# ConvNeXt block then selective scan on one core: the order of the loads between the first convolution and the MLP

## The chip, the cores and the metric

The kernel runs on one core of one Trainium2 chip, as one launch. The metric is the device time of that launch in microseconds; smaller is better. The time before the change is the median of three runs. A profile belongs to one further execution, which has its own time; the span in it runs from the first to the last instruction.

Names used below: TensorE (PE) multiplies matrices and PEld loads its weights, VectorE is DVE, ScalarE is ACT, GpSimd is POOL, and SP is SyncE, which issues most DMAs. A DMA moves data between the chip's main memory (DRAM here) and the on-chip memory; `SPq` in a profile is SP issuing one.

## The reference

The input `x` has 32 images of 96 channels and 56 x 56 pixels, float32. Two layers follow one another.

Layer 0 is a ConvNeXt block: a depthwise 7 x 7 convolution with bias, a layer norm over the 96 channels of each pixel, a small MLP (96 to 384, exact GELU, 384 to 96), a scale per channel, and the residual `+ x`:

```python
h = conv_depthwise_7x7(x) + conv_b                  # per channel
mu, var = mean(h, channels), var(h, channels)       # per pixel
h = (h - mu) * rsqrt(var + 1e-5) * ln_g + ln_b
h = gelu(h @ w1 + b1) @ w2 + b2                     # over channels
x = h * layer_scale + x
```

Layer 1 is a depthwise 5 x 5 convolution with SiLU, three small projections, and a scan along the 3136 pixels of each image with four states per channel. The change touches only layer 0.

## The kernel before

**Stages.** The kernel works in four stages with DRAM scratch tensors between them. *Convolution 1* goes over the 96 channels one by one; it writes the convolved rows to `conv1_d` and accumulates two statistics per pixel over the channels. *MLP* (the middle stage) goes over rows; it reads `conv1_d` and `x`, and writes `block_d`. *Convolution 2* goes over the channels again and writes `conv2_d`. *Scan* goes over images and halves of images.

**Layout.** The 32 images are two sets of 16. A row of a scratch tensor holds one image row of 16 images: 16 x 56 = 896 values (`COLS`). There are 2 x 56 = 112 such rows (`ROWS`), the first 56 for the first set. `conv1_d` is 96 channels x 112 rows x 896. The 896 are in two halves of 448 (`HALF`), the even and the odd pixels. `x` comes with the same rows, in pixel order.

**End of convolution 1.** For each channel after the first, `dt` is the difference to the first channel (L301); `acc1` sums it (L302) and `acc2` sums its square (L304), each 112 x 896. The statistics sit on 112 partitions as (half, row) and in the free dimension as (set of images, 448). After the last channel come L307 to L313: `sq` is `acc1` squared, `acc2` becomes the variance (L308, L311), ScalarE takes the root (L312, which loads an activation table first), and VectorE takes the reciprocal (L313). Two DMAs write it to `rstd_d` (L315), one for each half. The mean needs no step of its own: `w1` is centred when the weights are prepared.

**MLP.** The 112 rows are 28 groups of 4 (`RB`). A group needs seven tiles of three kinds: `r` is 1/std of its four rows, each row spread over 32 partitions (L345); `h` is the convolved rows for a block of 32 channels, with (row, channel) on 128 partitions and 896 in the free dimension, three blocks (L350); and `x` is the same piece of the input, loaded as four DMAs of one row each for every block (L354). So `load_rows` issues 1 + 3 + 12 DMAs. `normalise` multiplies one block of `h` by `r` in place on VectorE (L361). `hidden` is the first matrix product for one half of the pixels and 128 of the 384 hidden features (L371: 24 matmuls on 32-row tiles of the array) and GELU on ScalarE (L381). `result` is the second product (L390, 24 matmuls), to which VectorE adds bias and residual into the tile `o` (L401); after the second half POOL stores it to `block_d` with four DMAs (L413). Six `o` tiles are set to zero once at the start (L335), since a column of padding stays in them.

The loop runs over `k`, a half of a group at a time, with the second product one step behind the first. Loads run two groups ahead: groups 0 and 1 before the loop, group `n + 2` when `k` reaches group `n`. `h` and `x` have nine buffers each (three groups), `r` three.

**What sets the order.** A scheduler places instructions on each engine; those inside `pin(...)` keep the order of the program among themselves. In the MLP the normalises, matmuls and residual adds are pinned, the loads are not. In the built program SP has, for groups 0 to 2, `r`, then for each block `h` and four `x`; from group 3 on, the three `h` of a group, the `r` of the next group, and the twelve `x` of the group.

Waits come from two sources. A tile of a new pool stands on memory that the pool before has released, and waits for everything that used that pool. And SP's DMAs share eight semaphores in turn: a DMA waits, where needed, until the one eight places before it has landed.

The loads of `h` as the code has them:

```python
def rows_of(d, row, b):
    return d[CB * b : CB * b + CB, row : row + RB, :].rearrange("c r q -> r c q")
...
ht = pool.tile([128, COLS], F32, name=f"h_{n}_{d}", tag="h", bufs=9)
nc.sync.dma_start(ht, rows_of(conv1_d, row, d))
```

Of the kernel before, what the change touches and what calls it, by code (L numbers as in the profile page):

```python
# [8 lines left out]
F32 = mybir.dt.float32  # L9
AF = mybir.ActivationFunctionType  # L10
ALU = mybir.AluOpType
# [3 lines left out]
B, C, H, W = 32, 96, 56, 56  # L15
B2, BI = 2, 16
ROWS = B2 * H
COLS = BI * W
HALF = COLS // 2
# [20 lines left out]
RB = 4  # L40
# [6 lines left out]
def convnext_then_scan_kernel(  # L47
# [22 lines left out]
    nc = tc.nc  # L70
# [6 lines left out]
    conv1_d = dram.tile([C, ROWS, COLS], F32, name="conv1_d")  # L77
# [3 lines left out]
    rstd_d = dram.tile([ROWS, COLS], F32, name="rstd_d")  # L81
# [16 lines left out]
    eps_t = const.tile([128, 1], F32, name="eps_t")  # L98
# [42 lines left out]
    with tc.tile_pool(name="prep", bufs=1) as prep, tc.tile_pool(  # L141
        name="prep_ps", bufs=1, space=PSUM
# [8 lines left out]
        for i in range(3):  # L151
            for t in range(P1):
                j = 2 * t + 1 - i
# [11 lines left out]
        for k in range(QC):  # L165
            for f in range(QC):
                for t in range(2):
                    j = 4 * t + (k if k < 2 else k - 4) - f + K2 // 2
# [78 lines left out]
    def two(t):  # L247
        return t.rearrange("p (s q) -> p s q", s=2)

    with tc.tile_pool(name="c1", bufs=3) as pool, tc.tile_pool(  # L250
        name="c1k", bufs=1
    ) as keep, tc.tile_pool(name="c1_ps", bufs=4, space=PSUM) as psum:
        wts = [keep.tile([128, 2, H * P1], F32, name=f"wt1_{i}") for i in range(3)]
        xqs = [keep.tile([128, B2, BI, W2 + 3], F32, name=f"xq_{i}") for i in range(3)]
        for t in wts + xqs:
            nc.vector.memset(t, 0.0)
        first = keep.tile([ROWS, COLS], F32, name="first")
        acc1 = keep.tile([ROWS, COLS], F32, name="acc1")
        acc2 = keep.tile([ROWS, COLS], F32, name="acc2")
        nc.vector.memset(acc1, 0.0)  # L260
        nc.vector.memset(acc2, 0.0)

        def by_row(d, s):

            return d[:, s * PQ : (s + 1) * PQ].rearrange("(j m) q -> m j q", j=B2)

        for c in range(C):
            wv = toeplitz(taps1_d, wts[c % 3], K1, c, H)
            xt = pool.tile([128, COLS], F32, name=f"xt1_{c}", tag="xt")
            for j in range(B2):  # L270
                nc.sync.dma_start(xt[MP * j : MP * j + H], x[c, j * H : (j + 1) * H])

            xq = xqs[c % 3]
            for j in range(B2):
                xv = xt[MP * j : MP * j + H].rearrange("p (i r s) -> p s i r", i=BI, s=2)
                if j:
                    nc.vector.tensor_copy(xq[:H, j, :, 2 : W2 + 2], xv[:, 1])
                    nc.scalar.copy(xq[MP:KR, j, :, 1 : W2 + 1], xv[:, 0])
                else:
                    nc.gpsimd.tensor_copy(xq[:H, j, :, 2 : W2 + 2], xv[:, 1])  # L280
                    nc.scalar.copy(xq[MP:KR, j, :, 1 : W2 + 1], xv[:, 0])
            ps = psum.tile([ROWS, B2, 512], F32, name=f"ps1_{c}", tag="ps")
            for t in range(P1):
                for j in range(B2):
                    nc.tensor.matmul(  # L285
                        ps[:, j, :PQ].rearrange("p (i r) -> p i r", i=BI),
                        lhsT=wv[:KR, t],
                        rhs=xq[:KR, j, :, t : t + W2],
                        start=(t == 0),
                        stop=(t == P1 - 1),  # L290
                    )
            ht = first if c == 0 else pool.tile([ROWS, COLS], F32, name=f"ht_{c}", tag="ht")
            nc.scalar.activation(
                two(ht), ps[:, :, :PQ], AF.Identity, bias=c1b_t[:, c : c + 1], scale=1.0
            )
            for s in range(2):
                nc.gpsimd.dma_start(by_row(conv1_d[c], s), two(ht)[s * H : (s + 1) * H])
            if c:

                dt = pool.tile([ROWS, COLS], F32, name=f"dt_{c}", tag="dt")  # L300
                nc.vector.tensor_sub(dt, ht, first)  # L301
                nc.vector.tensor_add(acc1, acc1, dt)  # L302
                nc.scalar.activation(dt, dt, AF.Square)
                nc.vector.tensor_add(acc2, acc2, dt)  # L304

        sq = keep.tile([ROWS, COLS], F32, name="sq")
        nc.vector.tensor_mul(sq, acc1, acc1)  # L307
        nc.vector.scalar_tensor_tensor(  # L308
            acc2, in0=sq, scalar=-1.0 / C, in1=acc2, op0=ALU.mult, op1=ALU.add
        )  # L310
        nc.vector.tensor_scalar(acc2, acc2, 1.0 / C, 0.0, ALU.mult, ALU.max)  # L311
        nc.scalar.activation(acc2, acc2, AF.Sqrt, bias=eps_t[:ROWS], scale=1.0)  # L312
        nc.vector.reciprocal(acc1, acc2)  # L313
        for s in range(2):
            nc.sync.dma_start(by_row(rstd_d, s), two(acc1)[s * H : (s + 1) * H])  # L315

# [1 line left out]
    with tc.tile_pool(name="mlp", bufs=2) as pool, tc.tile_pool(  # L321
        name="mlp_h", bufs=3, space=PSUM
    ) as ps_h, tc.tile_pool(name="mlp_o", bufs=2, space=PSUM) as ps_o:
        pin = tc.keep_in_program_order
        blocks = C // CB
# [6 lines left out]
            pool.tile([128, QC, BI, QP], F32, name=f"o_{i}", bufs=1) for i in range(2 * blocks)  # L332
        ]
        for t in ots:
            nc.vector.memset(t, 0.0)  # L335

        def rows_of(d, row, b):
            return d[CB * b : CB * b + CB, row : row + RB, :].rearrange("c r q -> r c q")

        def load_rows(n):  # L340
            row = n * RB
            j, m = divmod(row, H)
            rt = pool.tile([128, COLS], F32, name=f"r_{n}", tag="r", bufs=3)
            rts[n] = rt
            nc.sync.dma_start(  # L345
                rt, bass.AP(rstd_d.tensor, rstd_d.offset + row * COLS, [[COLS, RB], [0, CB], [1, COLS]])
            )
            for d in range(blocks):
                ht = pool.tile([128, COLS], F32, name=f"h_{n}_{d}", tag="h", bufs=9)
                nc.sync.dma_start(ht, rows_of(conv1_d, row, d))  # L350
                hts[n, d] = ht
                xt = pool.tile([128, COLS], F32, name=f"x_{n}_{d}", tag="x", bufs=9)
                for i in range(RB):
                    nc.sync.dma_start(  # L354
                        xt[CB * i : CB * i + CB],
                        x[CB * d : CB * d + CB, j * H + H - 1 - m - i, :],
                    )
                xts[n, d] = xt

        def normalise(n, d):  # L360
            pin(nc.vector.tensor_mul(hts[n, d], hts[n, d], rts[n]))  # L361
# [56 lines left out]
        parts = groups * 2  # L418
        load_rows(0)
        load_rows(1)  # L420
        for d in range(blocks):
            normalise(0, d)
        for k in range(parts + 1):
            n = k // 2
            if k % 2 == 0 and n + 2 < groups:
                load_rows(n + 2)
            for f in range(3):
                if k < parts:
                    hidden(n, k % 2, f)
                if k:  # L430
                    result((k - 1) // 2, (k - 1) % 2, f)
                if k % 2 and n + 1 < groups:
                    normalise(n + 1, f)

# [335 lines left out]
```

## Time and profile before

| | |
|---|---|
| time, median of 3 runs | 3781.97 us (3781.74 to 3783.92) |
| the profiled execution, its own time | 3784.25 us |
| its span | 3782.4 us |
| granted TensorE clock, mean over the span | 0.824 |
| busy share: PE, DVE, ACT, POOL | 81, 74, 57, 60% |
| loads of `h` from `conv1_d` | 84 of 448 KB each |
| loads of `x` in the MLP | 336 of 112 KB each |
| loads of `r` from `rstd_d` | 28 of 448 KB each |

How to read it: a share of busy time is a mean over four stages with different limits. The page's slices (40 of 94.6 us) show them: TensorE is busiest up to about 1490 us, the end of the MLP, and VectorE after it. The timeline lists instructions in order of time with start, length, engine, line, operation, tiles (`out<-in`), and in brackets the idle time before it and what ended that wait. The line numbers are those of the kernel before. Busy time counts what the profile has for an engine; issuing a DMA isn't counted.

### The profile page before, as it was taken

The numbers are of one execution on the slowest core, as the hardware profiler recorded it, in microseconds if no ns is written. First come the engines' busy times: TensorE is split into PE (matmuls) and PEld (weight loads), VectorE is DVE, ScalarE is ACT, GpSimd is POOL, SyncE is SP. The second block draws the span as 40 slices with busy tenths as digits, with TensorE's granted clock in tenths as the row PEclk, the third lists the DMA queues.
The fourth block names the chain that finished last, engine by engine and source line by source line (L and its number), as shares of the span: only waits on it lengthen the run. The fifth ranks groups of instructions, "written<-read, shape, count | busy, mean of one in ns | idle before, by whom it ended". The sixth has DMA issues, their size and how long they took to land. (4 is left out here: it accounts for less than half of the span.)

```text
span 3782.4 us, 46657 instructions
## 1 busy us (share of the span) xinstructions
PE 3068.1 (81%) x17290; PEld 1274.2 (34%) x17290; DVE 2788.7 (74%) x1865; ACT 2169.2 (57%) x2037; POOL 2275.0 (60%) x1433
## 2 busy tenths in 40 slices
PE   7999995999999998876746777777777777787774
PEld 5777773333333333322212222222222222222221
DVE  5666664233333333999976999999999999999998
ACT  3555552333333333222217888888888878888884
POOL 2333331122222222677756898999889989988996
PEclk9999997999999999999976667666666666666666
DMA  5555553455555552877758877787778778777873
GB/s 155 165 168 168 165 168 102 153 170 162 159 159 161 164 163 79 228 215 216 217 137 274 273 257 263 267 277 252 260 273 272 253 264 274 267 259 261 276 252 113
DMA packets 303015, 790.71 MB, mean 209 GB/s; under 512 B 123972, under 2 KB 181124, under 8 KB 278116
## 3 DMA queue, kind: packets, MB, share of 16 engines
q1 hardware_dynamic: 252356, 630.77, 51.1%
q0 software_dynamic: 36096, 118.41, 11.4%
q10 hardware_dynamic: 14336, 38.54, 2.6%
q8 instruction: 137, 2.24, 0.2%
q14 instruction: 90, 0.74, 0.1%
HBM read 551.83 MB, written 235.74 MB: 208 GB/s over the span
## 5 line engine op out<-in xcount | busy, mean ns | idle before, releaser
L652 POOL TENSOR_TENSOR hs<-hs,ct 128x1568 f32<-128x1568 f32 x192 | 672.6, 3503 | 104.2 <-DVE hs L641 91.0
L625 POOL TENSOR_TENSOR rep<-rep,bt 128x1568 f32<-128x1568 f32 x192 | 674.5, 3513 | 13.6 <-DMA rep<-du_d 13.6
L381 ACT ACTIVATE g<-ph,b1p_t 128x896 f32<-128x896 f32 x336 | 320.3, 1004 | 512.4 <-PE ph L371 512.4
L401 DVE SCALAR_TENSOR_TENSOR o<-po,b2r_t,x 128x224 f32<-128x224 f32 x336 | 190.6, 609 | 572.7 <-PE po L390 572.7
L413 POOL DMA_DIRECT2D block_d<-o x336 | 183.1, 552 | 709.0 <-DVE o L401 621.9
L285 PE MATMUL ps<-xq,wt 120*112 120x448 f32 x1536 | 581.2, 540 | 14.3 <-POOL xq L280 14.3
L371 PE MATMUL ph<-h,w1r_t 32*128 32x448 f32 x4032 | 440.9, 560 | 60.2 <-DVE h L361 58.9
L285 PEld LDWEIGHTS ps<-xq,wt 120*112 120x112 f32 x1536 | 429.9, 280 | 165.2 <-POOL xq L280 14.5
L489 DVE COPY st<-yt 28x896 f32<-28x896 f32 x288 | 437.3, 1518 | 16.3 <-ACT yt L483 10.8
L556 PE MATMUL pz<-xs,wd_t 96*96 96x392 f32 x512 | 279.3, 712 | 187.8 <-ACT du L564 135.3
L472 PE MATMUL ps<-xq,wt 128*32 128x448 f32 x3072 | 311.3, 549 | 126.3 <-ACT yt L483 114.1
L390 PE MATMUL po<-g,w_t 128*32 128x448 f32 x4032 | 413.1, 543 | 0.0
L665 PE MATMUL py<-hs,sel_t 128*32 128x392 f32 x1536 | 330.1, 685 | 83.0 <-POOL hs L652 83.0
L632 DVE TENSOR_TENSOR_SCAN pv<-rep,pv 128x1568 f32<-128x1568 f32 x96 | 329.1, 3428 | 61.8 <-ACT rep L621 53.5
L601 PE MATMUL pk<-bn,pick_t 8*128 8x392 f32 x1024 | 290.1, 691 | 98.5 <-ACT y L675 80.7
L637 DVE SCALAR_TENSOR_TENSOR pv<-pv,rep 128x1568 f32<-128x1568 f32 x192 | 345.6, 1800 | 20.7 <-POOL hs L652 0.9
L632 DVE TENSOR_TENSOR_SCAN pv<-rep,carry_p,pv 128x1568 f32<-128x1568 f32 x96 | 334.9, 3489 | 9.8 <-DVE hs L641 1.3
L641 DVE TENSOR_TENSOR_SCAN hs<-rep,carry_h,pv 128x1568 f32<-128x1568 f32 x96 | 334.1, 3480 | 10.4 <-DVE pv L637 0.5
L641 DVE TENSOR_TENSOR_SCAN hs<-rep,pv 128x1568 f32<-128x1568 f32 x96 | 328.3, 3420 | 9.9 <-DVE pv L637 0.5
L619 ACT ACTIVATE rep<-rep,a_t 128x1568 f32<-128x1568 f32 x192 | 308.3, 1606 | 9.8 <-DMA rep<-du_d 9.4
L658 PE MATMUL py<-xs,dsm_t 96*96 96x392 f32 x512 | 304.9, 738 | 9.8 <-ACT ct L605 4.5
L620 ACT ACTIVATE rep<-rep,lift_t 128x1568 f32<-128x1568 f32 x192 | 307.6, 1602 | 6.3
(88 smaller groups left out, 3532.0 us busy)
## 6 DMA issues: line engine op xcount, KB each, us to landing
rep<-du_d SPq DMA_DIRECT2D x192, 1568.0 KB
du_d<-du SPq DMA_DIRECT2D x128, 588.0 KB
xq<-block_d SPq DMA_DIRECT2D x192, 225.0 KB
block_d<-o POOLq DMA_DIRECT2D x336, 120.0 KB, 5.7
xt<-in_x_dram SPq DMA_DIRECT2D x192, 196.0 KB
h<-conv_d SPq DMA_DIRECT2D x84, 448.0 KB
x<-in_x_dram SPq DMA_DIRECT2D x336, 112.0 KB
conv_d<-st POOLq DMA_DIRECT2D x96, 392.0 KB, 4.7
```

The costliest lines, as they stand in the source:

```text
L285: nc.tensor.matmul(ps[:, j, :PQ].rearrange("p (i r) -> p i r", i=BI), lhsT=wv[:KR, t], rhs=xq[:KR, j, :, t : t + W2], start=(t == 0), stop ...
L371: pin(nc.tensor.matmul(phs[i // 2][:, i % 2, :HALF], lhsT=w1r_t[rows, d, f * 128 : (f + 1) * 128], rhs=hts[n, d][rows, s * HALF : (s + 1) ...
L381: nc.scalar.activation(gt, ph[:, :, :HALF], AF.Gelu, bias=b1p_t[:, f : f + 1], scale=1.0)
L390: pin(nc.tensor.matmul(po[CB * i : CB * i + CB, :HALF], lhsT=w2_t[:, f, CB * d : CB * d + CB], rhs=gts[n, s, f, i // 2][:, i % 2], start=( ...
L472: nc.tensor.matmul(ps[RW * f : RW * f + RW, h, : B * QW].rearrange("p (b q) -> p b q", q=QW), lhsT=wv[:, f, t], rhs=xv[:, :, t : t + QW], ...
L489: copy(st[:, :, :, :, f], yt[RW * f : RW * f + QR].rearrange("p h (b q) -> p h b q", q=QW),)
L625: pin(nc.gpsimd.tensor_mul(ut, ut, bts[i // NG]))
L632: pin(nc.vector.tensor_tensor_scan(run, da, zero, carry_p[:, col : col + 1] if q else 1.0 / EPS, ALU.mult, ALU.add))
L637: pin(nc.vector.scalar_tensor_tensor(run, in0=run, scalar=1.0, in1=ut, op0=ALU.min, op1=ALU.mult))
L641: pin(nc.vector.tensor_tensor_scan(ht, da, run, carry_h[:, col : col + 1] if q else 0.0, ALU.mult, ALU.add))
L652: pin(nc.gpsimd.tensor_mul(ht, ht, cts[k]))
L665: pin(nc.tensor.matmul(py[g * DG : (g + 1) * DG, s, :BK], lhsT=sel_t, rhs=hss[k * NG + g][:, cols], start=False, stop=True, tile_position= ...
```

## The change

- `acc1` and `acc2` move to a pool of their own, `stats`, which stays open until the MLP is done (`front.close()`).
- `load_rows` now issues only the three `h` of a group. A new function `load_more` issues `r` and the twelve `x`. All these DMAs are pinned.
- `load_rows(0)` and `load_rows(1)` come first, then the norm's last steps, which are now in the MLP's pool (`sq` is a tile of it), then `load_more(0)` and `load_more(1)`. In the loop `load_more` follows `load_rows`.
- The reciprocal is taken in two halves of the free dimension, one for each set of 16 images. Each half is written to `rstd_d` with two DMAs, pinned: four in all.
- The zeroing of the `o` tiles moves from VectorE to POOL.

```diff
+    front = ctx.enter_context(ExitStack())
+    stats = front.enter_context(tc.tile_pool(name="stats", bufs=1))
+    acc1 = stats.tile([ROWS, COLS], F32, name="acc1")
+    acc2 = stats.tile([ROWS, COLS], F32, name="acc2")
...
-        acc1 = keep.tile([ROWS, COLS], F32, name="acc1")
-        acc2 = keep.tile([ROWS, COLS], F32, name="acc2")
...
-        sq = keep.tile([ROWS, COLS], F32, name="sq")
-        nc.vector.tensor_mul(sq, acc1, acc1)
-        nc.vector.scalar_tensor_tensor(
-            acc2, in0=sq, scalar=-1.0 / C, in1=acc2, op0=ALU.mult, op1=ALU.add
-        )
-        nc.vector.tensor_scalar(acc2, acc2, 1.0 / C, 0.0, ALU.mult, ALU.max)
-        nc.scalar.activation(acc2, acc2, AF.Sqrt, bias=eps_t[:ROWS], scale=1.0)
-        nc.vector.reciprocal(acc1, acc2)
-        for s in range(2):
-            nc.sync.dma_start(by_row(rstd_d, s), two(acc1)[s * H : (s + 1) * H])
...
-            nc.vector.memset(t, 0.0)
+            nc.gpsimd.memset(t, 0.0)
...
         def load_rows(n):
+            row = n * RB
+            j, m = divmod(row, H)
+            for d in range(blocks):
+                ht = pool.tile([128, COLS], F32, name=f"h_{n}_{d}", tag="h", bufs=9)
+                pin(nc.sync.dma_start(ht, rows_of(conv1_d, row, d)))
+                hts[n, d] = ht
+
+        def load_more(n):
             row = n * RB
             j, m = divmod(row, H)
             rt = pool.tile([128, COLS], F32, name=f"r_{n}", tag="r", bufs=3)
             rts[n] = rt
-            nc.sync.dma_start(
+            pin(nc.sync.dma_start(
                 rt, bass.AP(rstd_d.tensor, rstd_d.offset + row * COLS, [[COLS, RB], [0, CB], [1, COLS]])
-            )
+            ))
             for d in range(blocks):
-                ht = pool.tile([128, COLS], F32, name=f"h_{n}_{d}", tag="h", bufs=9)
-                nc.sync.dma_start(ht, rows_of(conv1_d, row, d))
-                hts[n, d] = ht
                 xt = pool.tile([128, COLS], F32, name=f"x_{n}_{d}", tag="x", bufs=9)
                 for i in range(RB):
-                    nc.sync.dma_start(
+                    pin(nc.sync.dma_start(
                         xt[CB * i : CB * i + CB],
                         x[CB * d : CB * d + CB, j * H + H - 1 - m - i, :],
-                    )
+                    ))
                 xts[n, d] = xt
...
         load_rows(0)
         load_rows(1)
+
+        sq = pool.tile([ROWS, COLS], F32, name="sq", bufs=1)
+        nc.vector.tensor_mul(sq, acc1, acc1)
+        nc.vector.scalar_tensor_tensor(
+            acc2, in0=sq, scalar=-1.0 / C, in1=acc2, op0=ALU.mult, op1=ALU.add
+        )
+        nc.vector.tensor_scalar(acc2, acc2, 1.0 / C, 0.0, ALU.mult, ALU.max)
+        nc.scalar.activation(acc2, acc2, AF.Sqrt, bias=eps_t[:ROWS], scale=1.0)
+        for i in range(B2):
+
+            nc.vector.reciprocal(acc1[:, i * HALF : (i + 1) * HALF], acc2[:, i * HALF : (i + 1) * HALF])
+            for s in range(2):
+                pin(nc.sync.dma_start(
+                    rstd_d[i * H : (i + 1) * H, s * HALF : (s + 1) * HALF],
+                    acc1[s * H : (s + 1) * H, i * HALF : (i + 1) * HALF],
+                ))
+        load_more(0)
+        load_more(1)
...
             if k % 2 == 0 and n + 2 < groups:
                 load_rows(n + 2)
+                load_more(n + 2)
...
+
+    front.close()
```

## The prediction

> **What bounds the kernel now.** I read the page's busy slices, then the timeline across the seam between the first convolution and the MLP, then the busy table by stretches. On the page:
>
> ```profile
> span 3782.4 us, 46657 instructions
> ...
> PE   7999995999999998876746777777777777787774
> ...
> PEclk9999997999999999999976667666666666666666
> ```
>
> A slice is 94.6 us. The MLP (about 671 to 1490 us) runs TensorE at 9 or more; the dip to 5 with a clock of 7 is the seam, at 567 to 662 us. The change acts there. The timeline of the seam (start, length, engine, line; the bracket is the idle time before and what ended it):
>
> ```profile
> 613.32 1.09 DVE L304 TENSOR_TENSOR acc<-acc,dt 112x896 f32<-112x896 f32 x1
> ...
> 618.65 5.75 DVE L313 RECIPROCAL acc<-acc 112x896 f32<-112x896 f32 x1 [2.45 <-ACT acc L312]
> 624.43 0.75 SPq L315 DMA_DIRECT2D rstd_d<-acc  x2
> 627.63 0.63 SPq L345 DMA_DIRECT2D r<-rstd_d  x1
> ...
> 641.95 1.09 DVE L361 TENSOR_TENSOR h<-h,r 128x896 f32<-128x896 f32 x1 [8.15 <-DMA h<-conv_d]
> ...
> 648.92 1.09 DVE L361 TENSOR_TENSOR h<-h,r 128x896 f32<-128x896 f32 x1 [5.88 <-DMA h<-conv_d]
> ...
> 655.78 1.09 DVE L361 TENSOR_TENSOR h<-h,r 128x896 f32<-128x896 f32 x1 [5.77 <-DMA h<-conv_d]
> ...
> 656.93 3.35 PE L371 MATMUL ph<-h,w1r_t 32*128 32x448 f32 x12 [4.99 <-DVE h L361]
> ...
> 658.87 1.28 ACT L381 ACT_TABLE_LOAD   x1 [40.26 <-PE ph L371]
> ...
> 661.22 7.44 PE L371 MATMUL ph<-h,w1r_t 32*128 32x448 f32 x48 [0.94 <-ACT g L381]
> ...
> 671.50 2.46 PE L390 MATMUL po<-g,w_t 128*32 128x448 f32 x24
> ```
>
> Read: the last matmul of the convolution ends at 608.9; the norm's chain ends with the reciprocal at 624.40; two writes of 1/std land by 627.6; then r, h (from 628.31) and x (from 628.90) of group 0 are issued. The three normalised blocks of group 0 wait for DMA until 641.95, 648.92 and 655.78, and only then can GELU begin (658.87). So the last 30 us of the seam are transfer time, and the norm only sets when the transfers start. The busy table, with columns PE, PEld, DVE, ACT, POOL (busy and count), clock, DMA share, GB/s:
>
> ```profile
> 741.00:747.00 6.00, 5.46 (x56) 1.85 (x56) 2.13 (x3) 1.91 (x2) 0.00 (x0) 1.00 0.25 95
> ```
>
> In this stretch h loads issued at 739.0 are on their way: a share of 0.25 at 95 GB/s is four of sixteen DMA engines at 24 GB/s each. From 671 us on no normalise waits for a DMA: a group takes 29.97 us (714.8 to 744.8 for the third block), its loads are issued 6 us and more ahead at first, 20 to 50 us later.
>
> **The Trainium skill.** *DMA: Bandwidth & Descriptors*, section "Why a DMA increments its semaphore by 16 and not by 1": a DMA issued from SP runs on k engines, k the largest number up to 16 that divides the slowest dimension of both patterns, and takes the lowest-numbered k; the other 16-k increments come at once. An h load has 128 partitions on one side and `r c q` with 4 rows outermost on the other: k = 4. r likewise 4; x (32 and 32) 16; the new 1/std writes (56 and 56) 14. The trace agrees: in its semaphore records h of block 0 has one early record (629.3) and just four late ones, 641.3 to 641.9; an x load has twelve records near 632.5 and four at 641.5 to 642.1; a 1/std write has fourteen. Same page, "Queues, rings and completion order": SP owns one ring on each engine, consumed in ring order. The trace agrees: those four late records of x come right after the h issued before it. *TensorE: Matmul & The Clock Gate*, Part 1: half clock until about one busy window of 3.4 us. Here the clock was 0.50 from 612.0 to 666.6, and the window from 663.2 was the first without a gap.
>
> **Part by part.** The changed program's order and waits, which can be read from its build, are used beside the durations above.
>
> 1. *h of groups 0 and 1 first.* Six h loads go to SP ahead of the 1/std writes. The first waits for the release of the convolution's pool: the last accumulate (ends 614.41) and the last conv1_d stores (records up to 613.9). So it issues at 614.5. All six use the same four engines. A load is 458,752 bytes: 4.6 us at 100 GB/s, 4.8 at the 95 above. With a start-up of 1.7 us (estimate, from the first landing record of the 1/std write, 626.2, after its issue at 624.43) the six end at 616.2 + 6 x 4.7 = 644.4. Nothing else competes then. Before, h and r of group 0 alone cost 9.4 (r_0, 627.63 to its last record at 637.0) + 4.9 + 7.0 + 6.9 us, the x loads between them included.
>
> 2. *The norm's steps later, with sq in the new pool.* sq was done in the shadow of the square (612.28); it now follows the last accumulate: +1.1 us. Two reciprocals of half length, 2.9 us each by 5.75/2. Chain: sq 614.5, L308's step 615.6, L311's 616.7, table load and sqrt 617.4 to 619.7, halves end at 622.7 and 625.6. Nothing waits for this (next point): there are 18 us of cover. Without that cover the 1.1 us would count, and the first half would give 2.9 us back.
>
> 3. *The 1/std writes, now four.* They stand behind six h loads in the rings of engines 0 to 3. Each brings 4 descriptors per engine (0.3 us), so the first two land about 1 us after the last h: 645.5, not 625.2. The halves buy nothing, since the second pair sits in the ring as well, ahead of r_0 on SP.
>
> 4. *r_0, then x.* r_0 waits for the first two writes: issue 645.6. Then 12 x. Up to seven x go out at once behind it, since SP's DMA semaphores come round every eight loads and the ones needed have landed. That is as before, when five or six x ran beside r_0 and it took 9.4 us; without disturbance 1.7 + 4.7 = 6.4. So r_0 lands between 652.0 and 655.0; I take 654.0, near the measured case.
>
> 5. *Start of the MLP.* All three h of group 0 have long landed, so the normalises follow at once (1.09 us each) and TensorE runs 24 matmuls without a gap: 8 cold ones took 1.88 us (timeline at 643.25 and 650.07), so 1.1 + 3 x 1.88 = 6.7 us. GELU's table load comes at 660.7, against 658.87: +1.8 us. In return the clock rises sooner: TensorE is busy without a gap from 655.1, so a full window is done by 658.6 to 662, not 666.6. Before, from 661.22 to 666.6, it did at half clock what takes half the time, 2.7 us too many; the GELU chain (0.95 us each, three PSUM buffers) hides part of it. I count -2.3 us. Sum at the first output matmul: +1.8 - 2.3 = -0.5 us; with r_0 at 652.0 it is -2.5.
>
> 6. *Later loads.* x_0 lands by 657, needed at about 674. r_1 comes behind 12 x: issue about 658, landing 665, needed at 675. h of group 2: issue 667, needed at 705. Nothing late.
>
> 7. *Steady groups.* Before, SP already ran h, then r of the next group, then x; now r of the same group follows h. It is needed over 20 us later: nothing. Pinning changes no more.
>
> 8. *Memsets of o on POOL.* On DVE they took 0.86 us each, six, in the wait for h. The timeline has no POOL entry from 612 to 691 us, so they find the engine free; even at several us each they end long before 674. What they may hold up on DVE is covered by the 18 us of point 2. Both ends nothing.
>
> Sum: -0.5 us, so span 3782. The profiled execution took 3784.25 beside its span, 2.3 above the median of 3781.97, so against the median: 3781.5.
>
> **Rivals.** *A, the queue takes the gain* (above): -4 to +5 us by the two bounds of h (4.6 or 4.9) and of r_0 (6.4 or 9.4). *B, faster: the transfers do overlap the norm.* If the h loads spread over sixteen engines, or the rings didn't hold the 1/std writes back, r_0 would issue at about 628 to 630, when the first three h are in, and land by 634 to 639; GELU starts 13 to 18 us sooner: 3764 to 3769. For it: the chain of waits then has only the norm in it. Against: four late records, 95 GB/s, and x landing behind h. A half-way case, with writes early but r_0 behind h of group 1: r_0 at 650, -4 us, within A. *C, slower: the h loads run below 100 GB/s,* so that 1/std is held longer. The price is six times the excess; from 5.9 us per load it passes the bound: 616.2 + 35.4 + 1.2 + 9.4 = 662.2, 8 us over A. For it: in the steady groups an h with its share of x and stores takes about 6 us. Against: here no x or store runs beside them. Price at 6.2 us: +10, so 3792. *D, the change does nothing* because the h loads stay behind the norm: excluded by the order, they stand first on SP.
>
> **How the numbers follow.** A 0.76, B 0.15, C 0.08, D 0.01. About 0.2% (7.6 us) is what a measurement of this kernel can tell from no change. Faster: B, 0.15. Slower: C, 0.08, and a little of A's tail, 0.09. Same: 0.76. The forecast is A's. A alone gives 3777 to 3787; B and C together are 0.23, and to leave out no more than 0.2 the range goes a little into both: 3772 to 3788.
>
> **What would show it.** Right: the six h loads issue from 614.5, and r_0 only at 644 to 647; the three normalises of group 0 follow each other without a gap at 652 to 656; DMA share near 0.25 at 95 to 105 GB/s through 618 to 644; first output matmul within 3 us of 671.5; clock up before 664. Wrong: r_0 issued before 635 (B), or a DMA share of 0.5 and more while h loads run. If normalises of group 1 or 2 wait for r, point 6 fails.

## The result, and the profile after

The changed kernel takes 3785.74 us (median, 3783.18 to 3787.97); the kernel before, run beside it on the same chip, 3782.30 us (3780.03 to 3787.0). The ratio is 1.0007, with a 95% interval of 0.9999 to 1.0015. That interval just includes no change, so this measurement doesn't tell one, though a loss of a few us is likelier than a gain. The forecast was 3781.5 us, "same" with 0.76. The profiled execution took 3786.44 us, its span is 3784.6 us. The page's lines that correspond to those shown of before:

```profile
span 3784.6 us, 46641 instructions
...
PE   7999994999999998876746777777777777777775
...
PEclk9999997999999999999976667666766776666666
```

The dip to 4 and a clock of 7 still stand in the same slice, the seam between the first convolution and the MLP. The timeline of that seam (start, length, engine, line of the changed kernel; in brackets the idle time before and what ended it):

```profile
615.51 13.57 SPq L336 DMA_DIRECT2D h<-conv_d  x6
615.64 5.56 POOL L326 MEMSET o<- 128x960 f32 x6 [3.09 <-DVE acc L306]
616.04 1.09 DVE L419 TENSOR_TENSOR sq<-acc 112x896 f32<-112x896 f32 x1 [0.66 <-DVE acc L306]
...
618.30 1.23 DVE L423 TENSOR_SCALAR acc<-acc 112x896 f32<-112x896 f32 x1
...
621.97 5.76 DVE L427 RECIPROCAL acc<-acc 112x448 f32<-112x448 f32 x2 [2.45 <-ACT acc L424]
629.13 6.33 SPq L429 DMA_DIRECT2D rstd_d<-acc  x4
646.51 0.52 SPq L344 DMA_DIRECT2D r<-rstd_d  x1
...
656.81 3.09 DVE L357 TENSOR_TENSOR h<-h,r 128x896 f32<-128x896 f32 x3 [29.08 <-DMA r<-rstd_d]
658.11 4.95 PE L367 MATMUL ph<-h,w1r_t 32*128 32x448 f32 x28 [48.24 <-DVE h L357]
...
662.45 1.28 ACT L377 ACT_TABLE_LOAD   x1 [40.51 <-issue]
...
664.81 4.23 PE L367 MATMUL ph<-h,w1r_t 32*128 32x448 f32 x24 [1.75 <-ACT g L377]
...
674.59 2.46 PE L386 MATMUL po<-g,w_t 128*32 128x448 f32 x24
```

The three waits for `h` of before (until 642, 649 and 656 us) have become one wait of 29.08 us for `r`, and it ends at 656.81, 1.0 us later than the last of the three did. The reciprocal's halves end at 624.9 and 627.7; `r` of group 0 isn't issued until 646.51, because the last parts of the 1/std writes land only then. The busy table by stretches, with columns PE, PEld, DVE, ACT, POOL (busy and count), clock, DMA share, GB/s:

```profile
622.00:628.00 6.00, 0.00 (x0) 0.00 (x0) 5.73 (x2) 0.00 (x0) 0.00 (x0) 0.50 0.26 103
628.00:634.00 6.00, 0.00 (x0) 0.00 (x0) 0.00 (x0) 0.00 (x0) 0.00 (x0) 0.50 0.27 108
634.00:640.00 6.00, 0.00 (x0) 0.00 (x0) 0.00 (x0) 0.00 (x0) 0.00 (x0) 0.50 0.38 147
640.00:646.00 6.00, 0.00 (x0) 0.00 (x0) 0.00 (x0) 0.00 (x0) 0.00 (x0) 0.50 0.25 102
```

From 622 to 646 us a quarter of the DMA engines is busy, at 102 to 108 GB/s, but for one stretch. The trace's semaphore records, which note when each engine has finished its part of a DMA, have the six `h` loads landing at 623.7, 628.2, 632.6, 637.1, 641.5 and 646.0, one every 4.45 us. Each 1/std write has fourteen parts. Ten of them land from 634.5 to 636.8, on engines that carry no `h` load; they are what is more in the stretch with 0.38 and 147 GB/s. The other four parts come only at 645.7 to 647.0, right behind the sixth `h`. *DMA: Bandwidth & Descriptors* of the Trainium skill, "Queues, rings and completion order", says that an engine consumes the descriptors (the single moves) of a ring, its queue for one issuing engine, in order; this is what it looks like when a small write stands behind six large loads.

### The profile page after: what moved, and what is told of

Read it like the earlier page. It is cut to its first block, busy times and chain, and to the rows that moved or that the text cites. A ratio compares the mean times of both kernels' runs of the same rounds, so it can differ in the third digit from the quotient of the medians.

```text
span 3784.6 us, 46641 instructions
## 1 busy us (share of the span) xinstructions
PE 3056.8 (81%) x17290; PEld 1269.7 (34%) x17290; DVE 2783.8 (74%) x1860; ACT 2168.5 (57%) x2037; POOL 2279.8 (60%) x1439
```

## Theory, rivals, and how the runs are read

The theory, that of the forecast: the change moves the `h` loads into the shadow of the norm, but all six use the same four DMA engines, and the writes of 1/std and then `r` stand behind them there. The rivals: the norm's chain is what ends last (then halves, memsets and the order of its steps matter); or loads of this kind are slow whatever engines they use.

One measure is used for all profiles below, since it leaves out the rest of the kernel: *the seam*, from the end of the last convolution matmul to the first output matmul (`po`). It is 62.60 us before (608.90 to 671.50) and 64.72 us after (609.87 to 674.59). From `po` to the end a profile has 3106.5 to 3111.5 us, in no order that follows the edits. That, and stage one (the first convolution) ending anywhere from 608.3 to 610.3, is why whole times of variants that differ by 1 to 2 us are not told apart here.

| kernel | time, us | before beside it | ratio, 95% | `r_0` issued | first normalise | seam |
|---|---|---|---|---|---|---|
| before | 3781.97 | | | 627.63 | 641.95 | 62.60 |
| changed | 3785.74 | 3782.30 | 0.9999 to 1.0015 | 646.51 | 656.81 | 64.72 |
| h of group 0 alone ahead | 3770.65 | 3781.82 | 0.9956 to 0.9981 | 632.92 | 643.67 | 51.62 |
| writes by ScalarE | 3781.57 | 3781.82 | 0.9989 to 1.0006 | 629.77 | 652.26 | 60.81 |
| split loads | 3760.52 | 3781.82 | 0.9929 to 0.9958 | 628.36 | 632.67 | 42.15 |
| one reciprocal | 3783.76 | 3781.82 | 0.9996 to 1.0014 | 645.92 | 655.38 | 63.55 |
| zeroing on VectorE | 3782.51 | 3781.57 | 0.9994 to 1.0011 | 644.39 | 654.03 | 63.34 |
| r of two groups ahead of x | 3782.91 | 3781.57 | 0.9995 to 1.0013 | 645.78 | 655.38 | 63.93 |
| r, then h of group 2, then x | 3781.17 | 3781.68 | 0.9990 to 1.0008 | 646.61 | 653.87 | 61.39 |
| early GELU table | 3780.77 | 3781.68 | 0.9991 to 1.0008 | 645.48 | 656.21 | 62.56 |
| before, with split loads | 3767.45 | 3782.11 | 0.9945 to 0.9975 | 628.05 | 634.14 | 47.97 |
| split, h of group 0 alone ahead | 3757.77 | 3782.11 | 0.9919 to 0.9953 | 626.34 | 630.26 | 39.08 |
| the same, one reciprocal | 3760.53 | 3782.11 | 0.9930 to 0.9959 | 630.38 | 634.45 | 41.15 |
| the same, zeroing on VectorE | 3762.91 | 3782.11 | 0.9933 to 0.9963 | 632.21 | 636.18 | 44.42 |

`r_0` is `r` of group 0, and so on.

## Is it the queue?

**Only h of group 0 ahead.** A shorter queue in front of the writes, nothing else:

```diff
         load_rows(0)
-        load_rows(1)
...
         load_more(0)
+        load_rows(1)
         load_more(1)
```

> Edit: the changed kernel, but only the three h loads of group 0 stand ahead of the norm; those of group 1 follow the x loads of group 0. Ring theory (1/std waits in SP's rings for every h load issued before it, 4.45 us each as in the changed kernel): three h loads fewer ahead, so r_0 issues at about 633 instead of 646.5, lands at 643.5, GELU's first table load comes at about 649 instead of 662.5; r of group 1 then lands at about 666 and may be 1 to 2 us late for its normalise. Time about 12 us under the changed kernel: 3774. Rival (the first two groups' bytes over four engines set the start, whatever the order): group 1 waits for what group 0 gains; time within 4 us of the changed kernel's 3785.7.

Measured: 3770.65 us. The timeline of this kernel:

```profile
621.86 5.76 DVE L426 RECIPROCAL acc<-acc 112x448 f32<-112x448 f32 x2 [2.45 <-ACT acc L423]
624.85 3.55 SPq L428 DMA_DIRECT2D rstd_d<-acc  x4
632.92 0.52 SPq L344 DMA_DIRECT2D r<-rstd_d  x1
...
643.67 3.10 DVE L357 TENSOR_TENSOR h<-h,r 128x896 f32<-128x896 f32 x3 [16.04 <-DMA r<-rstd_d]
...
661.37 2.46 PE L386 MATMUL po<-g,w_t 128*32 128x448 f32 x24
...
669.97 1.09 DVE L357 TENSOR_TENSOR h<-h,r 128x896 f32<-128x896 f32 x1 [4.86 <-DMA r<-rstd_d]
```

Three loads fewer in the queue are 3 x 4.45 = 13.4 us; `r_0` is issued 13.6 us sooner than in the changed kernel, and the seam is 13.1 us shorter. The norm's steps stand as they did. So the queue set the end, not the norm, and this part of the theory holds. The last line shows the price: `r_1` now comes late, and group 1 waits 4.86 us. That costs next to nothing: from the first to the last output matmul this kernel takes 828.1 us, the kernel before 828.0. The time came out 3.4 us under what the theory gave.

**The writes from another queue.** The four writes are issued by ScalarE, whose queue has nothing else in this stretch; all six `h` stay ahead:

```diff
-                pin(nc.sync.dma_start(
+                pin(nc.scalar.dma_start(
                     rstd_d[i * H : (i + 1) * H, s * HALF : (s + 1) * HALF],
```

> Edit: the changed kernel, but the four 1/std writes are issued by ScalarE instead of SP, so they are in another ring of the same engines. Ring theory: the first two land within 5 us of the first reciprocal (by 630), not at 646; r_0 is then issued at about 633 but stands behind the h loads of group 1 in SP's ring, lands at about 651 instead of 656.8, GELU 5 to 6 us sooner; time about 5 us under the changed kernel: 3780.5. Rival (the writes are slow because the four engines are full, whatever the ring): the writes land after 640 as before and the time stays at 3785.7 within 2 us.

Measured: 3781.57 us. The timeline of this kernel (`ACTq` is ScalarE issuing):

```profile
623.49 8.50 ACTq L429 DMA_DIRECT2D rstd_d<-acc  x4
629.77 2.64 SPq L344 DMA_DIRECT2D r<-rstd_d  x1
...
652.26 3.10 DVE L357 TENSOR_TENSOR h<-h,r 128x896 f32<-128x896 f32 x3 [26.00 <-DMA r<-rstd_d]
```

The writes no longer stand behind the loads: the last record of the first pair comes at 629.7, and `r_0` is issued 16.7 us sooner, or 15.3 counted from the end of the convolution, which came 1.5 us earlier in this profile. But it then stands behind `h` of group 1 itself, whose last load lands at 646.1, and the normalise comes only 3.1 us sooner, counted the same way; GELU was expected 5 to 6 us sooner. The seam is 3.9 us shorter than after the change: the other 0.8 is the clock, which didn't fall back in this run (last experiment). In kind this is the half-way case of the prediction ("r_0 at 650, -4 us"); in size it gained less, since against before the seam is 1.8 us shorter and the time is the same within the interval. Both the writes and `r` have to be free of the queue; freeing one moves the wait to the other.

**The loads on sixteen engines.** Every load of `h` and of `r` becomes four loads of one row each, 32 partitions against 32 channels, so that the division by which a DMA is spread gives sixteen engines instead of four (the Trainium skill, *DMA: Bandwidth & Descriptors*, "Why a DMA increments its semaphore by 16 and not by 1"):

```diff
-                pin(nc.sync.dma_start(ht, rows_of(conv1_d, row, d)))
+                for i in range(RB):
+                    pin(nc.sync.dma_start(
+                        ht[CB * i : CB * i + CB], conv1_d[CB * d : CB * d + CB, row + i, :]
+                    ))
...
-            pin(nc.sync.dma_start(
-                rt, bass.AP(rstd_d.tensor, rstd_d.offset + row * COLS, [[COLS, RB], [0, CB], [1, COLS]])
-            ))
+            for i in range(RB):
+                pin(nc.sync.dma_start(
+                    rt[CB * i : CB * i + CB],
+                    bass.AP(rstd_d.tensor, rstd_d.offset + (row + i) * COLS, [[0, CB], [1, COLS]]),
+                ))
```

> Edit: the changed kernel, but each h and each r load, in all groups, is four loads of one row (32 partitions) instead of one of four rows. Theory (four rows outermost put a load on four DMA engines; 32 against 32 puts it on sixteen): DMA share well over 0.25 while h loads run, the six h tiles land by about 630 instead of 646, the 1/std writes soon after the second reciprocal, r_0 by about 636, GELU's first table load at about 642 instead of 662.5: 20 us under the changed kernel, 3766. Rival (main memory or SP's issue is the limit, not the number of engines): the h tiles land after 640 and the gain is under 6 us.

Measured: 3760.52 us. The timeline of this kernel, then its busy table for the stretches in which `h` loads run:

```profile
625.31 1.67 SPq L434 DMA_DIRECT2D rstd_d<-acc  x4
628.36 1.69 SPq L348 DMA_DIRECT2D r<-rstd_d  x4
...
632.67 3.09 DVE L362 TENSOR_TENSOR h<-h,r 128x896 f32<-128x896 f32 x3 [6.46 <-DMA x<-in_x_dram]
```

```profile
616.00:622.00 6.00, 0.00 (x0) 0.00 (x0) 3.52 (x3) 2.32 (x2) 3.68 (x4) 0.50 0.89 241
622.00:628.00 6.00, 0.00 (x0) 0.00 (x0) 4.21 (x2) 0.00 (x0) 0.00 (x0) 0.50 0.94 236
```

The share goes from 0.26 to 0.9 and the rate from some 103 to 240 GB/s with the same bytes. The writes behind the six `h` have landed by 628.4, so `r_0` is issued 18 us sooner (16.6 counted from the end of the convolution), and the seam is 22.6 us shorter than after the change. The bracket names `x` because an `x` load's record on one of the eight shared semaphores came last; the last of the four `r` loads had landed at 632.35. The four engines are the cause, as the page says and as the landing records hinted before the change. Four times the engines gave 2.3 times the rate, not four.

**The kernel before with split loads.** The same edit, in the old order: `r`, then each `h` with its `x`, all behind the norm.

```diff
-                nc.sync.dma_start(ht, rows_of(conv1_d, row, d))
+                for i in range(RB):
+                    nc.sync.dma_start(
+                        ht[CB * i : CB * i + CB], conv1_d[CB * d : CB * d + CB, row + i, :]
+                    )
```

with `r` in the same way.

> Edit to the kernel before, nothing of the change: every load of h and r is four loads of one row each. Theory (loads on four engines are what the 30 us from the norm to the MLP consist of): the third normalise of group 0, at 655.8 us before, comes at about 643, and the time is about 3770 us. Rival (the norm and the latency of the chain write, r, h, x bind, not the engines): 3782 within 2.

Measured: 3767.45 us, 14.7 below before. The normalises of group 0:

```profile
634.14 1.07 DVE L366 TENSOR_TENSOR h<-h,r 128x896 f32<-128x896 f32 x1
...
638.10 1.09 DVE L366 TENSOR_TENSOR h<-h,r 128x896 f32<-128x896 f32 x1 [2.90 <-DMA h<-conv_d]
...
642.00 1.09 DVE L366 TENSOR_TENSOR h<-h,r 128x896 f32<-128x896 f32 x1 [2.81 <-DMA h<-conv_d]
```

They come 3.9 us apart instead of 6.9. So of the 24.3 us between before and the fastest kernel below, the split alone is 14.7, and early loads with all the rest 9.7. The change's own order, on split loads, is at 3760.52, some 7 us under this; without the split it gains nothing. What an early load is worth depends on what it queues in front of.

## What the other parts of the change are worth

**One reciprocal, in the changed kernel:**

```diff
-        for i in range(B2):
-
-            nc.vector.reciprocal(acc1[:, i * HALF : (i + 1) * HALF], acc2[:, i * HALF : (i + 1) * HALF])
+        nc.vector.reciprocal(acc1, acc2)
+        for i in range(B2):
             for s in range(2):
```

> Edit: the changed kernel, but one reciprocal over all 896 columns instead of two halves; the four writes stay. Ring theory: the first half of 1/std comes 2.9 us later and still 17 us before the rings are free; r_0 issue at 646.5 within 0.5 us, time 3785.7 within 2 us. Rival (the halves bring the first write forward on the path): r_0 and the time 2.9 us later, 3788.6.

Measured: 3783.76 us. The timeline of this kernel:

```profile
621.93 5.75 DVE L425 RECIPROCAL acc<-acc 112x896 f32<-112x896 f32 x1 [2.45 <-ACT acc L424]
628.53 6.34 SPq L428 DMA_DIRECT2D rstd_d<-acc  x4
645.92 0.52 SPq L344 DMA_DIRECT2D r<-rstd_d  x1
```

The first write goes out at 628.53, as in the changed kernel (629.13), where the first half had been ready since 624.9. SP was the reason: its first three `h` issues took 0.5 to 0.6 us each, the fourth 2.36, the fifth 4.98, the sixth 4.27, so it was still at work on the sixth when the half was done. The halves gain nothing here.

**The zeroing on VectorE, in the changed kernel:**

```diff
-            nc.gpsimd.memset(t, 0.0)
+            nc.vector.memset(t, 0.0)
```

> Edit to the changed kernel: the zeroing of the six o tiles stands on VectorE again, ahead of the norm's last steps, instead of on POOL. Theory (the queue hides what the norm does): the reciprocals end 4 to 6 us later, at about 632, still 14 us before the last h load has landed; r of group 0 is issued at 646.5 as before and the time is 3785.7 within 2. Rival (the norm sets the end): 4 to 5 us slower, 3790.

Measured: 3782.51 us. The timeline of this kernel:

```profile
625.96 5.76 DVE L427 RECIPROCAL acc<-acc 112x448 f32<-112x448 f32 x2 [2.45 <-ACT acc L424]
...
644.39 0.52 SPq L344 DMA_DIRECT2D r<-rstd_d  x1
```

The reciprocals end at 631.7, which is 5.4 us later than after the change if both are counted from the end of the convolution, and `r_0` is issued no later, so the queue covers this too. The time is 1.2 us below the band that was given for it; the seam is shorter by 1.4 us, one half of it before `r_0` is issued and one half in its landing, and that isn't explained.

**Without the queue.** The next kernel has split loads, only `h` of group 0 ahead, and `r_0` between the two halves' writes:

```diff
         load_rows(0)
-        load_rows(1)
...
             for s in range(2):
...
+            if i == 0:
+                load_r(0)
+        load_rows(1)
         load_more(0)
```

(`load_r` is the part of `load_more` that loads `r`, and `load_more` leaves out an `r` that is already loaded.)

> Edit to the changed kernel: every load of h and r is four loads of one row each; only the h of group 0 goes ahead of the norm's last steps; the four r loads of group 0 are issued between the two writes of the first half of 1/std and the two of the second; h of group 1 follows the writes. Theory (the queue on the four engines takes the gain, and the halves pay once it is gone): the reciprocal's first half ends at about 623.5 us, its writes land by 626, r of group 0 is issued there and lands by 629.5, so GELU's table load comes about 3 us sooner than with the split loads alone, and the time is 3757.5 us against 3760.5. Rival (the sixteen engines are now the bound, or SP's issues): no gain over the split loads, 3760.5 within 1.

Measured: 3757.77 us, ratio 0.9936 (0.9919 to 0.9953) to the kernel before: the fastest of all. The timeline of this kernel:

```profile
614.64 5.48 SPq L337 DMA_DIRECT2D h<-conv_d  x12
...
624.10 0.74 SPq L438 DMA_DIRECT2D rstd_d<-acc  x2
626.34 1.86 SPq L347 DMA_DIRECT2D r<-rstd_d  x4
628.31 0.93 SPq L438 DMA_DIRECT2D rstd_d<-acc  x2
...
630.26 3.09 DVE L367 TENSOR_TENSOR h<-h,r 128x896 f32<-128x896 f32 x3 [3.37 <-DMA rstd_d<-acc]
```

The first half of 1/std is written as soon as it is ready, and `r_0` is issued 2.2 us later; its last part lands at 630.13, just ahead of the normalise. (The bracket names the second half's write, which shares the semaphores.) Now the norm is the chain that ends last, and what it does must show. Two kernels undo one part each in this arrangement, with the edits to the reciprocal and to the zeroing that are shown above. First the reciprocal in one piece, with `r_0` still behind the first two writes:

> Edit: as the kernel with split loads, h of group 0 alone ahead and r of group 0 between the writes, but with one reciprocal of full length instead of two halves. It tells what the halves are worth once nothing queues in front of the writes. Theory: the first writes start when the whole reciprocal is done, 2.9 us later, and nothing hides that: 2.5 to 3 us slower than with the halves. Rival (the halves are worth nothing in any case): within 0.7 us of it.

Measured: 3760.53 us, 2.8 more. The reciprocal and the first normalise:

```profile
622.37 5.75 DVE L434 RECIPROCAL acc<-acc 112x896 f32<-112x896 f32 x1 [2.45 <-ACT acc L433]
...
634.45 3.09 DVE L367 TENSOR_TENSOR h<-h,r 128x896 f32<-128x896 f32 x3 [6.33 <-DMA rstd_d<-acc]
```

From the end of the convolution to this normalise it is 24.2 us, against 21.3 with halves: 2.9 us, one half of the reciprocal. The seam of this profile is only 2.1 us longer, because its clock didn't fall back. Then, with the halves, the zeroing on VectorE:

> Edit: as the kernel with split loads, h of group 0 alone ahead and r of group 0 between the writes, but the zeroing of the six o tiles stands on VectorE again, ahead of the norm's last steps, instead of on POOL. It tells what moving the zeroing is worth once the norm is on the path that sets the end. Theory: six times 0.86 us with some 0.15 us between them is 6 us on VectorE ahead of sq; less the 1.3 us that VectorE lost to POOL's zeroing, so 4 to 5 us slower. Rival (the zeroing finds room in a wait of VectorE): within 0.7 us of it.

Measured: 3762.91 us, 5.1 more. The timeline:

```profile
620.95 0.86 DVE L326 MEMSET o<- 128x960 f32 x1
621.73 1.03 DVE L428 TENSOR_TENSOR sq<-acc 112x896 f32<-112x896 f32 x1
...
636.18 3.09 DVE L367 TENSOR_TENSOR h<-h,r 128x896 f32<-128x896 f32 x3 [3.43 <-DMA rstd_d<-acc]
```

`sq` starts 6.7 us after the last accumulate instead of 0.7; 0.6 us of that comes back, since L432 takes 0.63 us here and 1.23 beside POOL's memsets. The normalise is 5.4 us later. So both parts that were worth nothing in the changed kernel are worth 2.8 and 5.1 us once nothing queues in front of the writes.

## Why r took so long, and what became of the clock

**Both r ahead of x.** In the changed kernel `r_0` takes 10.3 us from issue to normalise, an `h` in the queue 4.45. Is it `x`, issued right behind it?

```diff
+        load_r(0)
+        load_r(1)
         load_more(0)
         load_more(1)
```

> Edit to the changed kernel: r of groups 0 and 1 are both issued ahead of the x loads of group 0. It tells why r of group 0 took 10.3 us from issue to normalise where an h load in the queue took 4.45. Theory (the x loads, which go out on sixteen engines right behind r, share the four engines with it): without x beside it r of group 0 lands 6.5 to 7.5 us after its issue, so 3 to 3.7 us sooner, and the time is 3782.5 us. Rival (r is slow by itself, since 32 partitions read the same row): it lands as late as in the changed kernel, 3785.7 within 1.5.

Measured: 3782.91 us. `r_0` is issued at 645.78; the normalise:

```profile
655.38 3.10 DVE L362 TENSOR_TENSOR h<-h,r 128x896 f32<-128x896 f32 x3 [28.24 <-DMA r<-rstd_d]
```

It still takes 9.6 us, which by the expectation speaks for the rival; the time fits the theory's 3782.5, but at this size whole times don't tell. But the edit hadn't done what the expectation took for granted: `x` stands behind `r_1` on the four engines only, and on the other twelve it ran beside `r_0` as before (DMA share 1.03 at 650 to 652 us). And `r_1`, which reads one row 32 times just as `r_0` does, landed 4.7 us after `r_0`. So this run left the question open.

**r with nothing beside it.** Three `h` of group 2 go behind the two `r`, which keeps SP from issuing `x` until `r_0` has landed:

```diff
+        load_r(0)
+        load_r(1)
+        load_rows(2)
         load_more(0)
```

> Edit to the changed kernel: behind r of groups 0 and 1, the three h loads of group 2 are issued as well, and only then the x loads of group 0. All of these h and r loads use the same four engines, so SP can't issue x before r of group 0 has landed, and nothing runs on the other twelve engines beside it. It tells what the run with both r ahead of x left open: there x still ran on the other engines beside r, and r took 9.6 us. Theory (transfers on the other engines slow the four): r of group 0 lands 6.2 to 6.8 us after its issue, so 3.5 us sooner than in the changed kernel, and the time is 3782 us, if x doesn't come late for the first residual add. Rival (the first load behind the writes is slow by itself): 9.3 us or more from issue to landing, and 3785.7 within 2.

Measured: 3781.17 us. The timeline of this kernel:

```profile
646.61 1.08 SPq L343 DMA_DIRECT2D r<-rstd_d  x2
647.75 6.97 SPq L336 DMA_DIRECT2D h<-conv_d  x3
653.87 3.10 DVE L362 TENSOR_TENSOR h<-h,r 128x896 f32<-128x896 f32 x3 [25.74 <-DMA r<-rstd_d]
```

7.3 us from issue to normalise, 3.0 less than after the change. (`x` comes 1.4 us late for the first residual add, and TensorE doesn't wait for it.) Its landing records repeat the reading: `r_1` 4.5 us behind `r_0`, then the first `h` of group 2, which has `x` on the other engines beside it, 6.5 us, and the next two 4.7 and 4.8. So transfers on the other twelve engines slow these four, by 2 to 3 us for a load of 448 KB. That is the larger part; the landing, 7.2 us after the issue, is still 0.4 above the band given, because here a first load has 2.8 us ahead of its 4.45, not the 1.7 of the estimate.

**GELU's table ahead.** In the changed kernel TensorE stands still for 1.75 us behind GELU's table load, and the granted clock, which had risen at 661.5, is 0.50 again from 664.9 to 668.3, for 3.41 us, which is the step in which it changes in these profiles (a window).

```diff
         nc.scalar.activation(acc2, acc2, AF.Sqrt, bias=eps_t[:ROWS], scale=1.0)
+        early = pool.tile([ROWS, 1], F32, name="early", bufs=1)
+        nc.scalar.activation(early, acc2[:, :1], AF.Gelu, bias=eps_t[:ROWS], scale=1.0)
```

> Edit to the changed kernel: a GELU of one column, whose result nothing reads, stands right behind the square root on ScalarE, so that GELU's table is loaded at about 621 us, in the shadow of the loads, instead of at the first real GELU. It tells why the clock gave back so little: it rose at 661.5 us and fell again for one window, in which TensorE stood still behind the table load. Theory: the first GELU starts 1.28 us sooner, TensorE's gap shrinks from 1.75 us to about 0.5, the clock stays up and the eight to twelve matmuls behind run at full speed, 1 us more; first output matmul 1.5 to 2.5 us sooner after the first GELU than in the changed kernel, time 3783.5 us. Rival (the fall of the clock has to do with the window, not with the gap): 1.28 us and no more, with a second window at half clock.

Measured: 3780.77 us. The timeline of this kernel:

```profile
621.37 1.28 ACT L426 ACT_TABLE_LOAD   x1
...
656.21 3.10 DVE L357 TENSOR_TENSOR h<-h,r 128x896 f32<-128x896 f32 x3 [29.11 <-DMA r<-rstd_d]
657.51 8.53 PE L367 MATMUL ph<-h,w1r_t 32*128 32x448 f32 x52 [48.28 <-DVE h L357]
```

The busy table of one stretch, first of the changed kernel, then of this one (columns as above; the sixth is the clock):

```profile
664.00:668.00 4.00, 3.19 (x20) 1.70 (x24) 0.00 (x0) 1.65 (x2) 0.00 (x0) 0.62 0.58 117
```

```profile
664.00:668.00 4.00, 3.62 (x40) 1.72 (x36) 0.00 (x0) 2.21 (x3) 0.00 (x0) 1.00 0.48 98
```

TensorE now runs 8.53 us in one piece, and the clock, once up (663.6), stays up. From the first normalise to the first output matmul it is 15.58 us, against 17.78 after the change. The other runs divide the 2.2: where the clock fell back this stretch took 17.70 to 17.98 us (the changed kernel and eight others, TensorE's gap 1.63 to 1.78 us), where it didn't, 16.93 and 16.94 (writes by ScalarE, and the split loads with one reciprocal: gaps of 1.48 and 1.20 us). By that the fall costs some 0.85 us and the table load some 1.35. This is an estimate, since the clock also rose at different times in these runs, 4.4 to 7.4 us after the first normalise. From the first GELU to that matmul it is 9.39 us against 10.84, 1.45 sooner: that is just short of the band that the theory gave, and no second window at half clock came, against the rival.

## Why the prediction was right

Point by point, in the numbers of its steps.

1. *h first.* Right in kind; in size two errors mostly cancel, which is luck. Issue at 615.51 instead of 614.5, since stage one ended 1.0 us later in this profile. The first load took 8.2 us to land, 3.8 of them ahead of its own 4.45 (start-up estimated at 1.7): +2.1. Each load took 4.45, not 4.7: -1.5 for six. Last landing 646.0 instead of 644.4.
2. *The norm's steps.* The halves end at 624.9 and 627.7 (predicted 622.7 and 625.6): 1.0 us from stage one, 0.6 because `sq` starts 0.7 after the accumulate and not 0.1, 0.6 in L423. All of it covered, as said; the run with the zeroing on VectorE shows 5.4 us more covered as well.
3. *The writes.* Right: behind the sixth `h`, and the halves buy nothing. The two kernels with one reciprocal show both sides, nothing here and 2.8 us with the queue gone; the prediction had 2.9 for that.
4. *r_0.* Issue 646.51 against 645.6. Landing mis-sized: 10.3 us from issue to normalise, where the prediction took 8.4 "near the measured case" of 9.4, with bounds of 6.4 and 9.4. The upper bound itself was too low. Without `x` beside it, 7.3.
5. *Start of the MLP.* The clock's term was mis-sized. GELU's table load came 5.64 us after the first normalise, not 6.7, but with the late `r_0` that is 3.6 us later than before, where the prediction had 1.8. The credit for the clock was put at 2.3 us; from the table load to the first output matmul the changed kernel takes 12.14 us and the kernel before 12.63, a credit of 0.5. The clock rose before 664, but the prediction took it that it would stay up; it fell back for a window. So the sum was +3.1 us, not -0.5. From normalise to first output matmul it is 17.78 us instead of 17.0, which is about the 0.85 us of that fall.
6. *Later loads* and 7. *steady groups*. Right: no normalise of groups 1 to 3 waits for `r` or `h`, though `x_0` and `r_1` landed 4 to 5 us later than given, and first to last output matmul takes 828.1 us (before 828.0).
8. *Zeroing on POOL.* Nothing, as said, though not for free: 0.93 us each beside VectorE's steps, and a slower L423.

The sum at the first output matmul was 671.0; measured 674.59. The difference of 3.6 is 0.9 (stage one, the six loads and the writes), 1.9 (`r_0`), 0.8 (clock). From there to the end of the span the profile after has 3110.0 us, before 3110.9.

The range of A, -4 to +5 us, is wider than the two bounds that it names. A load at 4.6 or 4.9 us and `r_0` at 6.4 or 9.4 give -0.5 - 0.6 - 2.0 = -3.1 and -0.5 + 1.2 + 1.0 = +1.7. Measured were +3.1 at the first output matmul, or +2.1 without the later end of stage one, and +3.4 in the medians. So the mechanism, the queue that takes the gain, was right, and the runs above show it; that the time fell into the range is in part due to its width.

Of the rivals, B (transfers overlap the norm) described what split loads do: 3760.5 and 3757.8 us, a little below its 3764 to 3769. It was rejected for the right reason, four late records and 95 GB/s. C's price, from 5.9 us per load on, was not reached: 4.45. Of the marks to look for, normalises at 652 to 656 (656.8 to 659.9) and a first output matmul within 3 us of 671.5 (3.1) were missed, and the DMA share was near 0.25, at 102 to 108 GB/s, but for 634 to 640 us.

## What to carry to other kernels

Before moving loads ahead of a chain of small steps, ask which DMA engines they use and what has to pass through the same queue behind them: a large load placed early delays the small write and read that everything waits for. Look at the DMA share while such loads run: here 0.25 to 0.27 meant four engines of sixteen, and splitting the loads so that sixteen divides the outermost dimension on both sides was worth 14.7 us here before any reordering, and 24.3 with it. Parts of a change that measure as nothing may only be covered; take the cover away before dropping them.

## What the runs showed of the hardware that had not been expected

- Sixteen engines moved these loads at 236 to 241 GB/s with a share of 0.9, four at 102 to 108 with 0.26: 16 to 17 against some 25 GB/s for each busy engine.
- Loads on twelve engines slowed a load on the other four: 9.5 to 10.8 us from issue to normalise with `x` beside it, 7.3 without. The 1/std writes, which landed on ten of the others from 634.5 to 636.8, didn't: the `h` beside them took 4.44. Through what the loads slow each other stays open.
- SP's issues took longer the more such loads were under way: 0.5 to 0.6 us for each of the first three loads, 2.36, 4.98 and 4.27 for the next three, about the pace at which loads land (4.45). What stood behind on SP waited with them. That a full queue holds them up is likely, but no run isolates it.
- The granted clock fell back after a single gap of 1.63 to 1.78 us in the window after it rose (nine kernels, one profile each), and didn't after 1.20 and 1.48 (two). TensorE was busy for 48 to 52% of that window where the clock fell, and for 57 and 65% where it didn't; the runs don't tell which of the two counts. *TensorE: Matmul & The Clock Gate* of the Trainium skill, "Why this matters for your kernels", advises against gaps over about 3 us; here half of that was enough.
- A `tensor_scalar` on VectorE took 1.23 us while POOL zeroed tiles, and 0.63 without.
